# Four-layer conv stack on one core: TensorE's prices in the plan, a GpSimd share of the scan's products, and the first two images' preparation side by side

## The chip, the cores and the metric

The kernel runs on one core of a Trainium2 chip. The time is device microseconds from the start of an execution to its end. Four runs of the kernel before took 17,172.54 to 17,189.07 us, with a median of 17,181.15 us. A difference below 0.2% (about 34 us) is not told from no change here.

## The reference, cut to what matters

An image is a 128 x 56 x 56 block of float32; there are 32. Each passes four layers. Every layer normalises its input by groups of four channels and adds its result to the input.

```python
x = x + _L0(gn(x))   # attention-weighted 1x1 conv, then 3 dilated 3x3 depthwise convs, each through silu
x = x + _L1(gn(x))   # a cubic B-spline of every element, 10 coefficients
x = x + _L2(gn(x))   # linear attention over pooled 8x8 cells, then a 3x3 depthwise conv
x = x + _L3(gn(x))   # Mamba: layer norm, in-projection, short conv, selective scan, gate, out-projection

# inside _L3, for each position t and each of 256 inner channels d, 16 states n:
#   h[d,n] = exp(delta[t,d]*A[d,n]) * h[d,n] + delta[t,d]*xc[t,d] * B[t,n]
#   y[t,d] = sum_n h[d,n] * C[t,n]
```

The scan of layer 3 is the largest part, and the change touches its product `delta*xc*B`.

## The kernel before, in words

An image lies in SBUF as 128 channels x 3136 positions (tile `xt`). The positions are cut into NCH = 7 chunks of CH = 448. The scan of one chunk is cut into STEPS = 16 **steps**: DI = 2 halves of 128 inner channels, times NPAIR = 8 **pairs** of states. A step handles two states for 128 channels, as a tile of 128 partitions x 2 x 448. So an image has 112 steps and the run 3,584.

One step (class `Scan`, from line 1028) is made of these pieces:

- `b_rows`: one TensorE matmul spreads the two rows of B over the partitions, into the one PSUM buffer `pb` (pool `ps_bc`, one buffer).
- `c_rows`: the same for C. It runs for the first half alone; ScalarE copies it from PSUM to an SBUF tile `cb`, which both halves use.
- `decay`: two ScalarE exponentials write `da` to PSUM (three buffers).
- `state`: VectorE multiplies `du` (delta*xc, in SBUF) by `pb` into `h` (line 1074), then runs two scans over `h`. Tile `h` has three buffers.
- `products`: GpSimd multiplies `h` by `cb` into `hc` (two buffers); ScalarE keeps the last column of `h` in `last`.
- `add`: TensorE sums `hc` over the states into the PSUM tile `y`, two steps later.

While an image is scanned, layers 1 and 2 of the next one and layer 0 of the one after run between its steps. `Pieces` deals their generators out over the steps (`until_scan`, from line 1132, is layers 1 and 2 and the first layer norm; `first_layer`, from line 1125, is layer 0). Within a chunk, `gate` and `ssm_inputs` make the next chunk's `delta`, `du` and `xc`; the normed chunk goes through the tiles `xns` (three buffers, line 541).

The order on each engine is written out ahead by a planner (`Plan`, lines 95 to 325). Every instruction becomes a `Work` with a cost from `price` (line 163), a due time worked back from its step (`STEP` = 4.5 us for each), and what it reads and writes. `attempt` then goes through a simulated run: it takes the work that could start first on its engine, by due time among those near, and the engines' queues are issued in that order. On the chip every engine works through its own queue in order. `price` sets a float32 TensorE matmul of n columns at 1.8 ns a column and a float32r one at 0.5 ns a column.

Ahead of the loop (lines 1255 to 1262) three things are planned one after the other: layer 0 of image 0, its layers 1 and 2 with the first chunk's inputs, and layer 0 of image 1. Then a loop of five rounds follows, each with six images planned together, and a last part with two images.

All instructions are recorded through one helper, so nearly every line of the profile says L325; tiles tell them apart.

Of the kernel before, what the change touches and what calls it, by code (L numbers as in the profile page):

```python
# [19 lines left out]
P = 128  # L20
# [47 lines left out]
NB = DI * P // Q  # L68
NPAIR = NST // 2
STEPS = NPAIR * DI  # L70
AHEAD = 2
LAG = 3
FIRST, SECOND = 8, 4
# [7 lines left out]
class Work:  # L81


    __slots__ = ("engine", "calls", "reads", "writes", "cost", "bytes", "step", "ahead", "table", "due", "next",
                 "ready", "fresh")

    def __init__(self, engine, step, ahead):
        self.engine, self.step, self.ahead = engine, step, ahead
        self.calls, self.reads, self.writes = [], [], []
        self.cost = self.bytes = self.ready = self.due = 0.0  # L90
        self.table = None
        self.next, self.fresh = [], []


class Plan:
# [6 lines left out]
    RATE, LANDING = 2e5, 1.8  # L102
    TABLE = 1.28
    NEVER = 1e18
    PATIENCE = {"tensor": 0.5, "scalar": 0.9, "gpsimd": 0.6, "vector": 0.1, "sync": 0.0}

    def __init__(self, nc, tc):
# [55 lines left out]
    def price(self, w, engine, method, args, kw):  # L163

        n = args[0].free_size()
        if method == "dma_start":
            w.cost += 0.35
            w.bytes += 4 * n * args[0].partition_size()
        elif engine == "tensor":
            n = args[2].free_size() if method == "matmul" else n  # L170
            w.cost += max(0.06, n * (5e-4 if args[2].dtype == F32R else 1.8e-3))
        elif engine == "scalar":
            if method == "activation" and args[2] in (AF.Exp, AF.Tanh, AF.Ln):
                w.table = "ln" if args[2] == AF.Ln else "exp"
            columns = sum(isinstance(kw.get(k), bass.AP) for k in ("bias", "scale"))
            w.cost += 0.06 + 8.34e-4 * n + 0.09 * columns + 0.03 * (args[1].space != bass.MemoryType.PSUM)
        elif engine == "gpsimd":
            if n <= 8:
                w.cost += 0.52 if ALU.pow in args else 0.15
            else:  # L180
                slow = method != "tensor_scalar" or ALU.add not in args
                w.cost += 0.14 + n * (1.2e-3 if not slow else 2.12e-3 if method != "tensor_scalar" else 3.8e-3)
        elif method == "tensor_tensor_scan":
            w.cost += 0.11 + 2.085e-3 * n
        else:
            if method == "tensor_reduce" or method == "bn_stats":
                n = args[1].free_size()
            w.cost += 0.08 + 1.02e-3 * n
# [54 lines left out]
    def attempt(self, born, behind):  # L243
# [6 lines left out]
        left = dict(self.uses)  # L250
        free = {e: 0.0 for e in self.PATIENCE}
        ready = {e: [] for e in self.PATIENCE}
        slots, held, table, bus, first = {}, {}, None, 0.0, 0
        for name, (pool, tag, bufs) in self.tiles.items():
            slots[pool, tag] = [0.0] * bufs
            held[pool, tag] = []
# [5 lines left out]
        while len(out) < len(works):  # L262
            while done[first]:
                first += 1
            front = works[first].step + self.WINDOW
            best = None
            for e, cand in ready.items():
                for i in cand:
                    w = works[i]
                    if w.step > front:  # L270
                        continue
                    at = max(w.ready, free[e])
                    for name in w.fresh:
                        at = max(at, min(slots[self.tiles[name][:2]], default=self.NEVER))
                    if at >= self.NEVER:
                        continue
                    late = at - self.PATIENCE[e] * (w.ahead > 0)
                    if w.table and w.table != table:
                        late += 0.6

                    key = (max(late, free[e]), w.due, i)
                    if best is None or e != best[1] and at < best[3] or e == best[1] and key < best[0]:
                        best = (key, e, i, at)
            if best is None:
                full = [t for t in (self.tiles[n][:2] for n in works[first].fresh) if not slots[t]]
                behind.setdefault(first, []).append(max(born[n] for t in full for n in held[t]))
                return None
            key, e, i, at = best
            w = works[i]
            ready[e].remove(i)  # L290
            done[i] = True
            for name in w.fresh:
                t = self.tiles[name][:2]
                slots[t].remove(min(slots[t]))
                held[t].append(name)
            free[e] = at + w.cost
            if w.table:
                free[e] += self.TABLE * (w.table != table)
                table = w.table
            end = free[e]  # L300
            if w.bytes:
                bus = max(bus, end) + w.bytes / self.RATE
                end = bus + self.LANDING
            for name in self.used[i]:
                left[name] -= 1
                if not left[name]:
                    t = self.tiles[name][:2]
                    slots[t].append(end + self.HOP[e])
                    held[t].remove(name)
            for k in w.next + behind.get(i, []):  # L310
                v = works[k]
                waits[k] -= 1
                v.ready = max(v.ready, end + self.HOP[e] * (v.engine != e or e != "tensor"))
                if not waits[k]:
                    ready[v.engine].append(k)
            out.append((at, i))
        return [i for _, i in sorted(out)]

    def issue(self):
        order, works = self.order(), self.works  # L320
# [29 lines left out]
def tile_conv_stack(ctx: ExitStack, tc: tile.TileContext, out: bass.AP, x: bass.AP, w: dict):  # L350
# [12 lines left out]
    wide = pool("wide", 1)  # L363
    ssm = pool("ssm", 2)
    cbp = pool("cbp", NPAIR + 1)
    dramp = ctx.enter_context(tc.tile_pool(name="dramp", bufs=1, space=bass.MemoryType.DRAM))
    ps_mm = pool("ps_mm", 3, space=bass.MemoryType.PSUM)
    ps_bc = pool("ps_bc", 1, space=bass.MemoryType.PSUM)
# [169 lines left out]

    xts = [const.tile([P, L], F32, name=f"xt{k}") for k in range(3)]
    sts = [const.tile([P, NCH, 6], F32, name=f"st{k}") for k in range(2)]  # L540
    xns = [const.tile([P, CH + DCONV - 1], F32, name=f"xn{k}") for k in range(3)]
    dbls = [const.tile([P, CH], F32R, name=f"dbl{k}") for k in range(2)]
    xcs = [const.tile([P, DI, CH], F32, name=f"xc{k}") for k in range(2)]
    halves = [[const.tile([P, 2, CH], F32, name=f"{n}{k}") for k in range(3)] for n in ("delta", "du")]
# [444 lines left out]
    def ssm_inputs(xt, k, norm):  # L989

        dbl, xc = dbls[k % 2], xcs[k % 2]
        j, xn = k % NCH, xns[k % 3]
        for db in range(DI):
            ch = slice(db * P, (db + 1) * P)
            ps = psum()
# [16 lines left out]
            nc.vector.tensor_scalar(delta[:, db, :], ps, dtb[:, db : db + 1], 0.0, ALU.add, ALU.max)  # L1012
            yield 0.8
        nc.scalar.activation(du[:], du[:], AF.Exp, scale=-1.0)
        layer_norm(xt, xns[(k + 1) % 3], j + 1, norm if j + 1 < NCH else None, xn, du[:])
        nc.gpsimd.tensor_add(delta[:], delta[:], du[:])
        nc.gpsimd.tensor_mul(du[:], delta[:], xc[:])
        yield 4.0
# [9 lines left out]
    class Scan:  # L1028
# [3 lines left out]
        def __init__(self, xt, dst, last, k):  # L1032
            self.xt, self.dst, self.last, self.j, self.k = xt, dst, last, k % NCH, k
            self.dbl, self.xc = dbls[k % 2], xcs[k % 2]
            self.cbs, self.pbs, self.das, self.hcs = {}, {}, {}, {}

        def half(self, n):

# [16 lines left out]

        def b_rows(self, n):

            p = n % NPAIR
            self.pbs[n] = ps_bc.tile([P, 512], F32, tag="bc", name="pb")[:, :CH]
            self.both(self.pbs[n], B_ROW, p)  # L1060

        def decay(self, n):
# [3 lines left out]
            for i in range(2):  # L1066
                b = 2 * db + i
                nc.scalar.activation(self.das[n][i], delta[:, i, :], AF.Exp, scale=amat[:, b, p : p + 1])

        def state(self, n):  # L1070
            _, du = self.half(n)
            da = self.das.pop(n)
            h = ssm.tile([P, 2, CH], F32, tag="h", name="h", bufs=3)
            nc.vector.tensor_mul(h[:], du[:], self.pbs.pop(n).unsqueeze(1).to_broadcast([P, 2, CH]))
            for i in range(2):
                nc.vector.tensor_tensor_scan(
                    h[:, i, :],
# [3 lines left out]
                    ALU.mult,  # L1081
                    ALU.add,
                )
            self.h = h

        def products(self, n):
            h = self.h
            if self.j < NCH - 1:
                nc.scalar.copy(self.last[:, n, :], h[:, :, CH - 1])
            hc = ssm.tile([P, 2, CH], F32, tag="hc", name="hc", bufs=2)  # L1090
# [41 lines left out]
    def until_scan(b):  # L1132
# [4 lines left out]
        norm = carried[b % 2]  # L1137
        norm_weights(st, *norm)
        yield 5.0
        layer_norm(xt, xns[b * NCH % 3], 0, norm)  # L1140
        yield 5.0

    def first_inputs(b):
# [7 lines left out]
    class Pieces:  # L1151
# [12 lines left out]
            except StopIteration:  # L1164
                self.gen = None

        def finish(self, plan=None):
            while self.gen is not None:
                if plan is not None:
                    plan.at(plan.step + 1)  # L1170
                self.next()
            return self.taken

    xv = x.rearrange("b c l -> c b l")
# [3 lines left out]
    def images(first, count, ahead):  # L1178
# [18 lines left out]
        for b in range(count):  # L1197
# [5 lines left out]
            for j in range(NCH):  # L1203
                k = b * NCH + j
                if k == 0:
# [3 lines left out]
                        at(n, "c_rows")  # L1209
                    for n in range(2):  # L1210
                        at(n, "b_rows")
                    at(0, "decay")
                following = [gate(xns[k % 3])]
                if j + 1 < NCH:
                    following.append(ssm_inputs(xt, k + 1, carried[b % 2]))
                elif more:
# [2 lines left out]
                for n in range(STEPS):  # L1219
# [14 lines left out]
                    plan.at(g, FIRST)  # L1234
                    at(g + 2, "b_rows")
                    at(g, "state")
                    at(g + 1, "decay")
                    at(g, "products")
                    at(g + AHEAD, "c_rows")
# [14 lines left out]

    totals = [0.0, 0.0]
    plan.start()
    for b in range(2):
        totals[0] = Pieces(first_layer(xv[:, b : b + 1, :].squeeze(1), b)).finish(plan)
        if b == 0:
            totals[1] = Pieces(until_scan(0)).finish(plan)  # L1260
            Pieces(first_inputs(0)).finish(plan)
    plan.issue()
    with tc.For_i(0, B - 2, unroll) as i:
        images(i, unroll, True)
# [103 lines left out]
```

## Time and profile before

| | us |
|---|---|
| median of four runs | 17,181.15 |
| the profiled execution's own time | 17,196.77 |
| its span, first to last instruction | 17,194.7 |
| first scan product starts (the part ahead of the loop ends) | 504.9 |
| the two images behind the loop start their scans | 16,261.1 |
| the last image starts its scan | 16,766.5 |

The times of the last three rows are those at which VectorE starts the first `h<-du,pb` of the part. Between 504.9 and 16,261.1 us, 30 images take 525.2 us each on the mean. Mean granted TensorE clock: 0.886 of full speed.

In the profile, PE is TensorE's matmuls, PEld its weight loads, DVE is VectorE, ACT ScalarE, POOL GpSimd and SP the queue that issues the DMAs. A float32 matmul is two MATMUL instructions there. An operation is named out<-in by tiles: `hc<-h,cb` is the product with C. "A <- B" in a view of waits is time in which the engine of A stood idle until B ended.

### The profile page before, as it was taken

To read this page: it belongs to the slowest core of one execution; us is meant where nothing else is said; L and a number is where in the kernel's file an instruction comes from. 1 tells how busy PE (TensorE), PEld (TensorE's weight loads), DVE (VectorE), ACT (ScalarE), POOL (GpSimd) and SP (SyncE) were. 2 spreads that over 40 slices of the span, in tenths; PEclk is the share of its full clock that TensorE was granted. 3 is DMA by queue.
4 is the path that set the end of the run, shared out by engine and by line. 5 is a ranking of instruction groups with operands and counts; after the bars stand their busy time and mean duration, and the time that the engine had idled before them with its cause. 6 is when DMAs were issued, how large, how long until landed. Compare 5 with 4: busy or idle time off the path is not lost. (4 is left out here: it accounts for less than half of the span.)

```text
span 17194.7 us, 216067 instructions
## 1 busy us (share of the span) xinstructions
PE 14993.2 (87%) x68192; PEld 4864.7 (28%) x68192; DVE 14448.7 (84%) x17314; ACT 11730.0 (68%) x21127; POOL 10789.5 (63%) x6406
## 2 busy tenths in 40 slices
PE   5888998888988888988889888889888898888888
PEld 1222222222222222222222222222222222222222
DVE  2788888888888888888888888888888888888889
ACT  3666667766677666777666776667776667776675
POOL 1566666656666666666666666666666666666666
PEclk7888898989998888989889888899888999898887
DMA  4443443434433444434334434444343444343421
GB/s 106 104 96 94 101 98 85 97 88 98 106 90 85 97 95 99 99 85 97 92 93 106 94 80 96 95 102 98 86 96 90 94 106 94 84 97 93 95 54 31
DMA packets 986167, 1590.09 MB, mean 92 GB/s; under 512 B 175621, under 2 KB 611208, under 8 KB 984330
## 3 DMA queue, kind: packets, MB, share of 16 engines
q1 hardware_dynamic: 985002, 1576.06, 39.0%
q8 instruction: 548, 8.98, 0.2%
q14 instruction: 617, 5.05, 0.1%
HBM read 785.62 MB, written 173.18 MB: 56 GB/s over the span
## 5 line engine op out<-in xcount | busy, mean ns | idle before, releaser
L325 POOL TENSOR_TENSOR hc<-h,cb 128x896 f32<-128x896 f32 x3584 | 7482.2, 2093 | 5038.6 <-DVE h L325 2473.2
L325 DVE TENSOR_TENSOR_SCAN h<-da,last,h 128x448 f32<-128x448 f32 x6144 | 6807.8, 1137 | 627.8 <-ACT da L325 529.4
L325 ACT ACTIVATE da<-delta,alog 128x448 f32<-128x448 f32 x7168 | 4490.7, 633 | 2043.8 <-DVE h L325 1831.7
L325 DVE TENSOR_TENSOR h<-du,pb 128x896 f32<-128x896 f32 x3584 | 3831.7, 1069 | 428.6 <-PE pb L325 184.9
L325 PE MATMUL y<-hc,sums 128*64 128x448 f32 x14336 | 3933.0, 627 | 286.6 <-POOL hc L325 282.0
L325 PE MATMUL pb<-dbl,sel 64*128 64x448 f32 x3584 | 1842.9, 514 | 626.3 <-DVE h L325 585.3
L325 PE MATMUL mm<-xn,winT 128*128 128x448 f32 x3584 | 1786.0, 606 | 172.7 <-DVE sz L325 129.9
L325 PE MATMUL mm<-stack,dsT 96*32 96x448 f32 (+1 forms) x16128 | 1868.2, 573 | 59.9 <-DMA stack<-onesd 27.6
L325 ACT ACTIVATE hats<-stack,bia,scl 128x448 f32<-128x448 f32 x2688 | 1894.4, 755 | 12.8 <-DVE bia L325 10.0
L325 PE MATMUL mm<-hats,wspl 128*32 128x448 f32 x12544 | 1476.6, 574 | 130.7 <-DVE xt L325 68.5
L325 PEld LDWEIGHTS pb<-dbl,sel 64*128 64x128 f32 x3584 | 714.7, 199 | 2985.6 <-DVE h L325 1870.9
L325 PEld LDWEIGHTS y<-hc,sums 128*64 128x64 f32 x14336 | 800.1, 146 | 2064.6 <-issue 969.5
L325 ACT ACTIVATE t<-mm 128x448 f32<-128x448 f32 x1568 | 816.5, 536 | 788.7 <-PE mm L325 783.9
L325 ACT COPY cb<-mm 128x448 f32<-128x448 f32 x1792 | 927.9, 529 | 568.8 <-PE mm L325 471.5
L325 PE MATMUL mm<-dbl,sel 64*128 64x448 f32 x1792 | 874.1, 517 | 477.9 <-ACT cb L325 139.9
L325 ACT ACTIVATE hats<-hats,one 128x1344 f32<-128x1344 f32 x896 | 1261.3, 1408 | 1.2
L325 ACT COPY last<-h 128x2 f32<-128x2 f32 x3072 | 579.3, 189 | 817.0 <-DVE h L325 783.0
L325 DVE TENSOR_TENSOR_SCAN h<-da,h 128x448 f32<-128x448 f32 x1024 | 1062.9, 1071 | 54.8 <-ACT da L325 46.6
L325 POOL TENSOR_TENSOR xt<-xt,g 128x448 f32<-128x448 f32 x672 | 765.1, 1139 | 336.3 <-DVE g L325 331.1
L325 PEld LDWEIGHTS mm<-xn,winT 128*128 128x128 f32 x3584 | 614.2, 199 | 1029.2 <-issue 664.5
L325 PEld LDWEIGHTS mm<-stack,dsT 96*32 96x32 f32 (+1 forms) x16128 | 427.8, 112 | 1123.0 <-issue 862.5
L325 DVE SCALAR_TENSOR_TENSOR g<-t,mm 128x448 f32<-128x448 f32 x672 | 409.4, 609 | 398.9 <-ACT t L325 396.1
(187 smaller groups left out, 15888.4 us busy)
## 6 DMA issues: line engine op xcount, KB each, us to landing
stack<-padded SPq DMA_DIRECT2D x2688, 264.0 KB
stack<-xt SPq DMA_DIRECT2D x3584, 56.0 KB
delta<-delta SPq DMA_DIRECT2D x1792, 112.0 KB
du<-du SPq DMA_DIRECT2D x1792, 112.0 KB
padded<-yc SPq DMA_DIRECT2D x224, 264.0 KB
padded<-yc SPq DMA_DIRECT2D x256, 231.0 KB
xt<-x_dram SPq DMA_DIRECT2D x224, 224.0 KB
out_dram<-xt SPq DMA_DIRECT2D x224, 224.0 KB
```

What stands on the lines that cost most here:

```text
L325: call()
```

## The change

Four things change together.

1. `ASIDE = (4,)`: for pair 4 of the eight, `b_rows` makes B's rows once for both halves, in a general PSUM buffer, and ScalarE copies them to an SBUF tile `bb` (new pool, one buffer). GpSimd then multiplies `du` by `bb` for that pair, in place of VectorE's multiply of `du` by `pb`. These are two of a chunk's 16 products.
2. The product leaves `state` for a method of its own, `inputs`. It is listed for step g+1 right behind `state` of step g, so for every pair it is recorded, and due, one step earlier.
3. TensorE's prices: a float32r matmul costs 0.16 us more, a float32 one 0.02 us + 1.75 ns a column, both with full clock. `Plan.run` keeps a load for each window of 3.413 us and lets TensorE work at half speed in a window that follows one with too little load.
4. Layer 0 of image 1 is no longer planned behind the rest of the part ahead of the loop, but dealt out between the pieces of `until_scan(0)`.

The tiles `xns` go from three to two, which makes room for `bb`. The core of the diff:

```diff
+ASIDE = (4,)
+    GATE, BUSY = 3.413, 1.27
@@ Plan.price
-            w.cost += max(0.06, n * (5e-4 if args[2].dtype == F32R else 1.8e-3))
+            w.load += n * (1.9e-4 if args[2].dtype == F32R else 7.5e-4 * 2) * args[-1 if method != "matmul" else 1].partition_size() / P
+            w.cost += 0.16 + 5e-4 * n if args[2].dtype == F32R else max(0.22, 0.02 + 1.75e-3 * n)
@@ Plan.attempt
-            free[e] = at + w.cost
+            free[e] = self.run(at, w, loads) if e == "tensor" else at + w.cost
+    def run(self, at, w, loads):
+        left = w.cost
+        while left > 0.0:
+            k = int(at / self.GATE)
+            speed = 1.0 if loads.get(k - 1, 0.0) >= self.BUSY else 0.5
+            stay = min((k + 1) * self.GATE + 1e-9 - at, left / speed)
+            loads[k] = loads.get(k, 0.0) + stay * speed * w.load / w.cost
+            at, left = at + stay, left - stay * speed
+        return at
@@ tiles
+    bbp = pool("bbp", len(ASIDE))
-    xns = [const.tile([P, CH + DCONV - 1], F32, name=f"xn{k}") for k in range(3)]
+    xns = [const.tile([P, CH + DCONV - 1], F32, name=f"xn{k}") for k in range(2)]
@@ Scan.b_rows
-            p = n % NPAIR
+            db, p = divmod(n, NPAIR)
+            if p in ASIDE:
+                if db == 0:
+                    ps = psum()
+                    self.both(ps, B_ROW, p)
+                    self.bbs[p] = bbp.tile([P, CH], F32, tag="bb", name="bb")
+                    nc.scalar.copy(self.bbs[p][:], ps)
+                return
@@ Scan
+        def inputs(self, n):
+            _, du = self.half(n)
+            h = self.hs[n] = ssm.tile([P, 2, CH], F32, tag="h", name="h", bufs=3)
+            if n % NPAIR in ASIDE:
+                nc.gpsimd.tensor_mul(h[:], du[:], self.bbs[n % NPAIR][:].unsqueeze(1).to_broadcast([P, 2, CH]))
+            else:
+                nc.vector.tensor_mul(h[:], du[:], self.pbs.pop(n).unsqueeze(1).to_broadcast([P, 2, CH]))
         def state(self, n):
-            _, du = self.half(n)
-            h = ssm.tile([P, 2, CH], F32, tag="h", name="h", bufs=3)
-            nc.vector.tensor_mul(h[:], du[:], self.pbs.pop(n).unsqueeze(1).to_broadcast([P, 2, CH]))
+            h = self.hs[n]
@@ Pieces
-        def finish(self, plan=None):
+        def finish(self, plan=None, beside=None):
+            start = beside and beside.taken - self.taken / 2
...
+                while beside and beside.gen is not None and beside.taken - start < self.taken / 2:
+                    beside.next()
@@ images
                     at(g, "state")
+                    at(g + 1, "inputs")
                     at(g + 1, "decay")
@@ ahead of the loop
-    for b in range(2):
-        totals[0] = Pieces(first_layer(xv[:, b : b + 1, :].squeeze(1), b)).finish(plan)
-        if b == 0:
-            totals[1] = Pieces(until_scan(0)).finish(plan)
-            Pieces(first_inputs(0)).finish(plan)
+    layer0s = [Pieces(first_layer(xv[:, b : b + 1, :].squeeze(1), b)) for b in range(2)]
+    totals[0] = layer0s[0].finish(plan)
+    totals[1] = Pieces(until_scan(0)).finish(plan, layer0s[1])
+    Pieces(first_inputs(0)).finish(plan, layer0s[1])
+    layer0s[1].finish(plan)
```

## The prediction

> **What bounds the kernel now.** I read the page's engine totals first. TensorE (PE) and VectorE (DVE) are nearly level, and neither is full.
>
> ```profile
> PE 14993.2 (87%) x68192; PEld 4864.7 (28%) x68192; DVE 14448.7 (84%) x17314; ACT 11730.0 (68%) x21127; POOL 10789.5 (63%) x6406
> ```
>
> An average hides stages, so next I cut an image in the middle of the loop (the 14th) into its seven chunks, at the first scan of each, and asked for busy time in these stretches. Columns: stretch and length, then busy us of PE, PEld, DVE, ACT, POOL, the granted TensorE clock, DMA share, GB/s.
>
> ```profile
> 7333.10:7398.10 65.00, 49.67 (x161) 16.28 (x162) 59.55 (x78) 42.62 (x79) 44.06 (x25) 0.79 0.28 71
> 7398.10:7477.40 79.30, 63.42 (x253) 20.17 (x250) 67.43 (x85) 60.42 (x108) 47.53 (x30) 0.84 0.21 50
> 7477.40:7558.60 81.20, 75.97 (x361) 21.69 (x361) 64.57 (x72) 70.76 (x124) 58.08 (x35) 0.90 0.44 104
> 7558.60:7630.10 71.50, 64.45 (x363) 20.04 (x355) 62.74 (x74) 61.00 (x109) 53.23 (x33) 1.00 0.49 112
> 7630.10:7709.90 79.80, 71.48 (x325) 28.93 (x322) 66.97 (x82) 44.61 (x86) 43.15 (x27) 0.81 0.31 71
> 7709.90:7792.30 82.40, 81.19 (x452) 25.14 (x450) 69.89 (x81) 44.91 (x91) 46.10 (x27) 1.00 0.62 147
> 7792.30:7857.40 65.10, 57.61 (x233) 18.40 (x233) 59.44 (x70) 41.08 (x68) 44.96 (x29) 0.90 0.46 103
> ```
>
> So the bound moves: VectorE in chunks 1 and 7 (92% and 91% busy), TensorE in chunk 6 (99%, at full clock), and no engine alone in chunks 2 to 5 (VectorE 80 to 88%, waiting in turn on the others). GpSimd is never over 75%. The waits say the same: GpSimd mostly waits for VectorE's scans or for a free `hc`, and VectorE's largest wait is for ScalarE's `da`.
>
> ```profile
> POOL hc L325 <- DVE h L325: 2473.2, 1249, 6.9
> POOL hc L325 <- PE y L325: 1866.5, 804, 12.4
> ...
> DVE h L325 <- ACT da L325: 576.0, 440, 4.4
> ```
>
> Last, the part ahead of the loop. Layer 0 of image 0 ends at about 134 us; its layers 1, 2 and first inputs run to about 398; layer 0 of image 1 fills the rest up to the first scan at 504.9.
>
> ```profile
> 134.00:398.00 264.00, 166.09 (x747) 53.45 (x747) 46.07 (x100) 124.92 (x165) 42.99 (x38) 0.67 0.23 57
> 398.00:505.00 107.00, 74.15 (x526) 23.36 (x526) 22.95 (x41) 19.61 (x37) 28.85 (x26) 0.80 0.90 204
> ```
>
> **Part 1: two images ahead of the loop.** The second stretch, 107 us, moves beside the first. Does it fit? TensorE's work at full clock is 166.09 x 0.67 + 74.15 x 0.80 = 171 us, ScalarE's 145, the DMA engines' 0.23 x 264 + 0.90 x 107 = 157, all below 264. By their yields, layer 0 counts 90 units and `until_scan` 212, and one unit is dealt out for two, so all of layer 0 is dealt out by 180 of 212. SP's transfers of layer 0 (the same stack loads, in the same number) join a queue that was nearly idle. The first stretch is a chain of latencies (ScalarE's functions, a slow-clock matmul, VectorE, and again), and in-order queues will hold it up here and there. I take 107 less 17 for that: **-90 us**. Ends: -40, if more than half of it comes back as waits, and -120, if the busier TensorE also gets more clock than 0.67.
>
> **Part 2: VectorE's relief and what pays for it.** The rows:
>
> ```profile
> L325 POOL TENSOR_TENSOR hc<-h,cb 128x896 f32<-128x896 f32 x3584 | 7482.2, 2093 | 5038.6 <-DVE h L325 2473.2
> L325 DVE TENSOR_TENSOR h<-du,pb 128x896 f32<-128x896 f32 x3584 | 3831.7, 1069 | 428.6 <-PE pb L325 184.9
> L325 PE MATMUL pb<-dbl,sel 64*128 64x448 f32 x3584 | 1842.9, 514 | 626.3 <-DVE h L325 585.3
> L325 ACT COPY cb<-mm 128x448 f32<-128x448 f32 x1792 | 927.9, 529 | 568.8 <-PE mm L325 471.5
> ```
>
> A chunk loses 2 VectorE products, 2 x 1.069 = 2.14 us, and 1 of 16 `pb` matmuls net (two go, one for `bb` comes), 0.51 us. It gains one ScalarE copy, 0.53 us by `cb`'s row, and two GpSimd products of the same shape as `hc`, 2 x 2.093 = 4.19 us. In all VectorE sheds 448 x 1.069 = 479 us and GpSimd takes 938.
>
> What is on the path differs by chunk. Chunks 1 and 7: VectorE sets the pace, all 2.14 counts. Chunk 4 (88%): 1.5. Chunks 2 and 5 (85 and 84%): about half, 1.1 each. Chunk 3, where ScalarE stands at 87% and TensorE at 94%: 0.4. Chunk 6 is TensorE's: its 0.5. Sum 4.3 + 1.5 + 2.2 + 0.4 + 0.5 = 8.9 us an image. Against it stands ScalarE's copy, 0.5 in chunk 3 alone and hidden where ScalarE is at 55 to 85%; if that cover went, 3.7 an image.
>
> GpSimd also disturbs VectorE. `dm<-mv,mg`, on one column, takes 139 ns in the median, 520 on the mean and up to 1,783; where it overlaps a GpSimd operation its mean is 1,462, elsewhere 137. Its likes (`vv`, `attr`, `pooled`, `ab`, `att`) together lose about 166 us in the run. GpSimd's busy time grows by 9%, so 9% more of that: 14 us, 0.5 an image. The Trainium skill has the rule (SBUF — State Buffer, "SBUF: two separate sides"): VectorE and GpSimd take one port pair by turns, for a whole instruction, when VectorE reads two SBUF inputs. By the rule alone every GpSimd microsecond is a possible block and the change is bad; but the products and scans take one input from PSUM, and the scans' spread (1,097 to 1,153 ns over the run, with GpSimd busy or not) shows none of it. By it the sum would still be the 14 us.
>
> Net 8.9 - 0.5 - 0.5 = 7.9 an image, over 31 images 245, and in the last image, where VectorE alone is pressed, 7 x 2.1 = 15: **-260 us**. Ends: 0, if it is all swallowed by other waits, and -479.
>
> **Part 3: a new wait.** VectorE's scan of pair 4 waits for a GpSimd product that stands in GpSimd's in-order queue behind `hc` products, and these behind a free `hc` or a side addition. Behind the scan on VectorE stand the next product and all side work, so ScalarE's `da` and TensorE's `pb` wait too. In time for it: `du` and `bb` are ready steps earlier; the `h` buffer comes free with `hc` of three steps before; two steps (9.3 us) ask GpSimd for three such products, 6.3 us, and about 2 x 0.9 of side work, 8.1 in all. No row shows this wait. The nearest is VectorE's product waiting for `hc` to free `h`: 73 us in the run, 62 times, 1.2 us each. Ends: 0, and a whole GpSimd operation each time, 448 x 2.09 = +936. I take 1.2 us for one in twenty of the 448: **+27 us**.
>
> **Part 4: the plan's prices and the earlier product.** They change no instruction, only the order. In an image (14,497 to 15,019 us) VectorE stood idle 72 us, 38 of them because a TensorE result came later than the order assumed, directly or through ScalarE (`g<-t`, `xt<-mm`, `h<-pb`, `delta`, `sz`, `rden` and so on). A plan that knows TensorE at half clock can place these consumers later; all of it would be 31 x 38 = -1,180. On the other side, a wrong order costs; how much an order's luck is worth is seen in the loop's images, whose orders are the same in every round: from first scan to first scan they take 520.0 to 526.3 us (the last of each round aside): +-3 us, +-100 over the run. I take -2 an image, nearest to that row: **-62 us**. The Trainium skill (TensorE: Matmul & The Clock Gate, "What's actually happening") says the clock's window runs free of the kernel. If so the planned windows lie beside the real ones and this part is 0; the spread just named would agree.
>
> **At nothing:** `xns` with two buffers. The norm that overwrites a buffer waits for the `gate` of the same chunk, dealt out some six steps before, about 28 us; without that cover GpSimd's queue, `hc` with it, would stand until TensorE reads. `bb`'s one buffer is rewritten some seven steps after its last reader. The earlier listing of the products adds none.
>
> **Sum:** -90 - 260 + 27 - 62 = -385. The profiled execution took 17,196.8, so 16,812; it lies 15.6 above the median of the runs, so **16,796 us**.
>
> **The rivals.**
> - *More comes through* (chance 0.20). VectorE's relief counts whole (-479), part 1 gives -90, and better prices 5 us an image (-155): -724, 16,457. For it: VectorE has the most work that no clock can speed up. Against: 99% TensorE in chunk 6.
> - *Only the part ahead of the loop gains* (0.18). Chunks are set by TensorE and by waits in turn, VectorE's 2 us only lengthen its idle time: 17,181 - 90 = 17,091. For it: in that image's chain of waits TensorE holds half of the time and VectorE's `h` 15%.
> - *GpSimd's product comes late* (0.12, slower). In its queue it stands behind an `hc` that waits for `y`, which is GpSimd's second largest wait. The gains without part 3 are 412 us, so the point of decision is 412/448 = 0.92 us a product. At 1.25 us, 560 - 412 = +148: 17,329.
> - *Nothing to measure* (0.05): part 1 gives its low end and the loop a little back, 17,160.
>
> The forecast itself has 0.45, with 16,650 to 16,950 as its own range. The range for 8 in 10 leaves out about half of the first rival and most of the slower one: 16,450 to 17,215. Faster by over 0.2% (34 us, about what a measurement tells from no change): 0.45 + 0.20 + 0.18 = 0.83; within 0.05; slower 0.12.
>
> **What would show it.** The first scan starts near 415 us instead of 505 (part 1). Chunks 1 and 7 of an image fall from 65 to about 63 us, chunk 6 stays at 82 (part 2). A wait of VectorE's `h` for a GpSimd product, absent now, stays below 50 us (part 3). `g<-t`, `xt<-mm` and `h<-pb` waits fall somewhat, and the clock stays near 0.89 (part 4). The prediction is wrong if chunk 6 or the mixed chunks move by over 5 us either way, or if that new wait is in hundreds of microseconds.

## The result, and the profile after

The changed kernel took 17,202.91 us (median of 40 runs) against 17,179.94 us before (60 runs): the ratio is 1.0013, with a 95% interval from 1.0009 to 1.0017. That is below the 0.2% that was to count, but on the slow side: three parts that were each meant to gain gave nothing together. The profiled execution's span is 17,208.2 us, so span and median agree.

The engine totals of the changed kernel, in the page's form:

```profile
PE 14938.3 (87%) x67968; PEld 4900.1 (28%) x67968; DVE 14084.5 (82%) x16866; ACT 11830.9 (69%) x21351; POOL 11698.2 (68%) x6854
```

VectorE's busy time fell by 364 us and GpSimd's grew by 909. The products by themselves did as worked out: VectorE's `h<-du,pb` fell by 474 us and GpSimd's `h<-du,bb` took 938. But other operations of VectorE ran 110 us longer, and VectorE's idle time, span less busy, grew from 2,746 to 3,124 us. All of the 364 became waiting.

The part ahead of the loop, cut at the same times as before (the first scan product now starts at 441.5 us instead of 504.9):

```profile
134.00:398.00 264.00, 195.05 (x1277) 65.43 (x1269) 55.60 (x103) 126.75 (x178) 64.97 (x56) 0.76 0.56 128
398.00:443.00 45.00, 20.05 (x43) 9.61 (x44) 6.03 (x14) 17.18 (x24) 8.66 (x9) 0.67 0.17 39
```

The first stretch now holds layer 0 of image 1 as well: 1,277 matmuls instead of 747, at a clock of 0.76 instead of 0.67. What it was to hide is hidden, and 45 us of the old work are left over behind it. So 63 us are won here.

The seven chunks of the same image as before (the 14th), with the same columns:

```profile
7317.10:7389.70 72.60, 54.85 (x166) 18.02 (x166) 61.40 (x77) 45.06 (x83) 48.42 (x27) 0.74 0.26 66
7389.70:7466.60 76.90, 64.58 (x263) 19.94 (x259) 62.73 (x81) 63.80 (x114) 55.33 (x33) 0.87 0.24 62
7466.60:7545.80 79.20, 72.48 (x344) 21.79 (x342) 62.16 (x71) 67.80 (x119) 58.50 (x36) 0.87 0.42 97
7545.80:7620.20 74.40, 67.46 (x360) 21.00 (x359) 61.00 (x71) 63.07 (x113) 57.53 (x35) 0.93 0.47 107
7620.20:7696.10 75.90, 71.19 (x325) 29.17 (x325) 64.29 (x80) 44.86 (x87) 49.60 (x30) 0.84 0.34 79
7696.10:7774.70 78.60, 78.16 (x445) 24.53 (x444) 66.30 (x80) 43.72 (x89) 46.99 (x27) 1.00 0.62 145
7774.70:7838.20 63.50, 56.87 (x238) 18.27 (x234) 59.15 (x68) 41.64 (x69) 50.30 (x31) 0.92 0.48 111
```

The first chunk is the one to look at. It was VectorE's, at 92%; it went from 65.0 to 72.6 us, and VectorE is idle for 11 us of it. Chunks 2, 3, 5, 6 and 7 gained about 2 to 4 us, chunk 4 lost 3. This image as a whole even took 3 us less than before (521.1 against 524.3), so it does not show the loss; on the mean over the 30 images of the loop chunk 1 rose from 65.4 to 73.5 us, and it stands at 70.4 in e4 below, without a product on GpSimd. Over the loop, from its first scan to the first scan behind it, the time rose from 15,755 to 15,838 us: +83, which eats the 63. (The times 16,261.1 and 16,766.5 in the table of the kernel before are those of first scans; the products before them start at 16,257.2 and 16,765.3.)

VectorE's waits (us, times, longest), first before, then in the changed kernel:

```profile
DVE h L325 <- PE pb L325: 184.9, 176, 3.6
...
DVE sz L325 <- PE y L325: 126.3, 112, 5.1
...
DVE h L325 <- POOL hc L325: 73.3, 62, 1.5
```

```profile
DVE h L339 <- ACT da L339: 732.9, 593, 5.8
...
DVE h L339 <- PE pb L339: 333.2, 256, 5.0
...
DVE sz L339 <- PE y L339: 272.3, 145, 5.4
DVE h L339 <- POOL hc L339: 229.5, 184, 3.5
...
DVE h L339 <- POOL h L339: 45.1, 53, 1.9
```

The last line is the wait that the prediction was afraid of, VectorE's scan for GpSimd's product, and it is small. The line above it stood at 73.3 us before. It is VectorE's own product that waits for GpSimd's `hc`, that is, for a free buffer of `h`. This line gave theory D, which was put on record before e5. Two other waits grew by as much, by some 150 us each: the product's for `pb`, and that of `sz`, the gate, for `y`, the sum of `hc`.

**Theory D.** In the plan, the GpSimd product needs only `du`, `bb` and a free `h` buffer, all there early, and GpSimd has idle time. So the planner places it far ahead of its scan. From then on it holds one of the three `h` buffers, and VectorE works with two or one. To see it, the k-th `h<-du,bb` was matched with the k-th scan of pair 4: from the end of the product to the start of the scan 12.5 us pass on the mean; for the second half of a chunk's steps the median is 16.6 us, for the first half only 1.1. The last image shows it best, since no other image's layers run beside the scan there. This is its second chunk in the timeline of the changed kernel (start, length, what, idle before):

```profile
16830.41 2.08 POOL L339 TENSOR_TENSOR h<-du,bb 128x896 f32<-128x896 f32 x1
...
16838.44 2.19 DVE L339 TENSOR_TENSOR_SCAN h<-da,last,h 128x448 f32<-128x448 f32 x2
...
16840.78 2.08 POOL L339 TENSOR_TENSOR hc<-h,cb 128x896 f32<-128x896 f32 x1 [6.12 <-DVE h L339]
...
16842.89 1.09 DVE L339 TENSOR_TENSOR h<-du,pb 128x896 f32<-128x896 f32 x1 [0.38 <-POOL hc L339]
...
16844.01 2.19 DVE L339 TENSOR_TENSOR_SCAN h<-da,last,h 128x448 f32<-128x448 f32 x2
...
16846.38 2.08 POOL L339 TENSOR_TENSOR hc<-h,cb 128x896 f32<-128x896 f32 x1 [3.52 <-DVE h L339]
```

The product made at 16,830.41 is the one of step 12; its scan starts at 16,878.7, 46 us later. The product of step 4 was made at 16,824.0, for a scan at 16,850.6. Two of three buffers are taken, so product, scan and `hc` follow each other one by one. The step from scan to scan takes 5.6 us, where such steps without the held buffers take 3.6.

**Rivals**, on record before e1. A: the order that the new prices make costs what the relief gains. B: the relief is swallowed by other waits wherever it falls. C: GpSimd's product disturbs by its own 2.09 us in front of `hc`.

### The profile page after: what moved, and what is told of

Its sections match the earlier page's. It is cut to its first block, busy times and chain, and to the rows that moved or that the text cites. A ratio compares the mean times of both kernels' runs of the same rounds, so it can differ in the third digit from the quotient of the medians.

```text
span 17208.2 us, 214516 instructions
## 1 busy us (share of the span) xinstructions
PE 14938.3 (87%) x67968; PEld 4900.1 (28%) x67968; DVE 14084.5 (82%) x16866; ACT 11830.9 (69%) x21351; POOL 11698.2 (68%) x6854
## 5 line engine op out<-in xcount | busy, mean ns | idle before, releaser
L339 PE MATMUL y<-hc,sums 128*64 128x448 f32 x14336 | 4049.7, 649 | 401.4 <-POOL hc L339 398.9
L339 DVE TENSOR_TENSOR h<-du,pb 128x896 f32<-128x896 f32 x3136 | 3357.6, 1071 | 648.7 <-PE pb L339 333.2
L339 PE MATMUL pb<-dbl,sel 64*128 64x448 f32 x3136 | 1620.2, 517 | 686.5 <-DVE h L339 651.3
L339 PE MATMUL mm<-dbl,sel 64*128 64x448 f32 x2016 | 975.7, 528 | 476.7 <-DVE g L339 102.8
L339 PEld LDWEIGHTS pb<-dbl,sel 64*128 64x128 f32 x3136 | 629.8, 201 | 2578.7 <-DVE h L339 1516.9
L339 POOL TENSOR_TENSOR h<-du,bb 128x896 f32<-128x896 f32 x448 | 938.0, 2094 | 213.5 <-DMA out_dram<-xt 69.5
L339 PEld LDWEIGHTS mm<-dbl,sel 64*128 64x128 f32 x2016 | 390.9, 211 | 1568.4 <-issue 300.0
```

The source lines that it names most:

```text
L339: call()
```

## The experiments

All times are medians. "Half clock" is the time that TensorE's clock stood at half in the profiled run, summed from the clock's records.

| run | what | us | half clock, us |
|---|---|---|---|
| | before | 17,180 | 3,932 |
| | changed | 17,203 | 4,319 |
| e1 | before + interleaved start | 17,142 | 3,905 |
| e2 | before + new prices | 17,189 | 3,987 |
| e3 | before + GpSimd products, earlier listing | 17,338 | 4,449 |
| e4 | changed, no GpSimd products | 17,101 | 4,082 |
| e5 | changed, products in step order | 16,973 | 3,491 |
| e6 | e4 with two `h` buffers | 17,301 | 4,150 |
| e7 | e4 with the rule of e5 | 17,105 | 4,058 |
| e8 | before + earlier listing | 16,845 | 3,215 |
| e9 | e5 with the old prices | 17,300 | 4,678 |
| e10 | e5, GpSimd one step early | 17,156 | 4,060 |
| e11 | e5 with two pairs on GpSimd | 17,243 | 4,679 |
| e12 | before, one price 3% off | 17,173 | 3,860 |
| e13 | e8, one price 3% off | 17,371 | 4,112 |
| e14 | changed, one price 3% off | 17,218 | 4,192 |
| e15 | e5, one price 3% off | 16,943 | 3,768 |
| e16 | e4, one price 3% off | 17,128 | 3,975 |
| e17 | e9, one price 3% off | 17,377 | 4,853 |
| e18 | e8 + interleaved start | 16,725 | 3,027 |

### The parts one by one (e1 to e4)

e1 takes the change's part ahead of the loop into the kernel before:

```diff
-    for b in range(2):
-        totals[0] = Pieces(first_layer(..., b)).finish(plan)
...
+    totals[1] = Pieces(until_scan(0)).finish(plan, layer0s[1])
```

> The kernel before with the interleaved part ahead of the loop alone. In the changed kernel the first scan product starts at 441.5 us instead of 504.9, and this part is planned by itself, so both theories expect the first scan 55 to 75 us earlier (the plan's prices differ between the two, which may shift it by some us), the loop's rounds at 3,147 to 3,158 us as before, and a time of -55 to -75 us, about 17,115.

Ratio 0.9979 (0.9970 to 0.9988), -38 us. The first scan came 69 us earlier. Its VectorE, ScalarE and GpSimd queues from the first scan on hold the same operations in the same order as before, and yet its loop took 15,784 instead of 15,755 us. Both expectations held for the part itself and were off by 17 us for the whole.

e2 puts `price`, `run` and `free[e] = self.run(...)` of the change into the kernel before.

> The kernel before with TensorE's new prices and the modelled clock alone; no instruction changes but the order. Theory A (the order that the new prices make costs what VectorE's relief gains): slower by 200 us or more, 17,380 and up. Theory B (the relief is swallowed by other engines' waits wherever it falls): within 60 us of before. Theory C (GpSimd's product disturbs): within 60 us of before, or faster as forecast by up to 62.

Ratio 1.0007 (0.9998 to 1.0016): no difference. A fell; the prices alone make no worse order, nor a better one.

e3 takes GpSimd's products, the earlier listing and two `xns`, and leaves the prices and the start as they were.

> The kernel before with GpSimd's products, the earlier listing of all products and two norm buffers; old prices, old part ahead of the loop. Theory A: faster by about 260, 16,920. Theory B: within 60 us of before. Theory C: slower by 80 us or more, 17,260 and up, with a wait of VectorE or TensorE on GpSimd that the kernel before has not.

Ratio 1.0091 (1.0076 to 1.0106), +158 us. Theory C expected this, but e8 and e13 below have the same kernel without GpSimd's products at 16,845 and 17,371 us, so with the old prices GpSimd's part cannot be told from the order's. e4 takes the GpSimd products out of the changed kernel:

```diff
-ASIDE = (4,)
+ASIDE = ()
```

> The changed kernel with no pair on GpSimd (an empty list of pairs): interleaved start, new prices, earlier listing and two norm buffers stay, VectorE makes all products again. Theory A: slower than the changed kernel by the relief, 260, so 17,460. Theory B: within 60 us of the changed kernel, 17,140 to 17,260. Theory C: faster than the changed kernel by 80 or more, 17,120 or less.

Ratio 0.9950 (0.9936 to 0.9963), 17,101 us. So 102 us of the changed kernel come with GpSimd's products. A and B fell; C remained, and D, which was stated after this run, gives the same.

### Too early or too long (e5 to e7, e10)

e5 adds one rule to the planner, and no instruction:

```diff
         behind = {}
+        hs = sorted(born[n] for n, (pool, tag, _) in self.tiles.items() if n in born and (pool, tag) == ("ssm", "h"))
+        for i, k in zip(hs, hs[1:]):
+            behind.setdefault(i, []).append(k)
```

> The changed kernel, with one rule more in the plan: a product of du is placed behind the product of the step before it, on whichever engine. Instructions are the same. Theory D (in the changed kernel the GpSimd product is placed up to 12 steps early, sits in one of the three h buffers all that time and leaves VectorE two or one): the lead of the GpSimd product falls from 12.5 us on the mean to under 5, VectorE's waits of h for hc fall from 230 us to under 90, and the time falls below the version without GpSimd products (17,101), to 16,950 to 17,080. Theory C2 (GpSimd's own 2.09 us, in front of hc, make y and the side work late wherever they stand): 17,180 to 17,240, about the changed kernel, and VectorE's waits for hc stay.

Ratio 0.9874 (0.9859 to 0.9889), 16,973 us. GpSimd does the same 448 products, now 0.66 us ahead of their scans on the mean, and the kernel is 230 us faster than the changed one and 128 faster than e4. VectorE's waits in e5:

```profile
DVE h L342 <- POOL hc L342: 156.3, 124, 4.1
...
DVE h L342 <- POOL h L342: 98.5, 132, 1.7
```

The wait for `hc` fell from 230 only to 156, not under 90 as expected, where e4 without GpSimd's products has 114; the wait for the product itself rose. VectorE's wait of `sz` for `y` fell from 272 to 72 (e14, the changed kernel in another order, has 111). The time was as D expected and not as C2, the form of C in the expectation.

Two rivals of the held buffer are left. An early product also stands in front of an `hc` in GpSimd's queue and so makes `y` late, and the rule of e5 takes that away too. And other operations of VectorE run longer in the changed kernel: of the 228 us between the two profiled spans, VectorE's busy time makes up 95 (14,084.5 against 13,989.6, with the same instructions) and its idle time 133.

The last image, cut from its first scan to the first scan of its seventh chunk, shows the cost without other images' layers. Before, changed kernel, e5:

```profile
16766.50:17131.30 364.80, 316.31 (x768) 96.39 (x767) 332.62 (x349) 206.76 (x420) 234.59 (x124) 0.76 0.15 34
```

```profile
16768.20:17141.30 373.10, 300.90 (x767) 95.05 (x766) 325.62 (x339) 213.83 (x430) 262.18 (x138) 0.78 0.14 34
```

```profile
16567.20:16917.50 350.30, 291.74 (x762) 90.78 (x762) 319.99 (x337) 214.03 (x428) 259.32 (x137) 0.80 0.15 36
```

With the product too early the six chunks take 373.1 us. They take 373.1 and 379.7 in e14 and e3 too, the other two versions that place it early, and 346 to 365 in all kernels that do not. So in the last image the cost of placing it early shows in every order. The gain does not: in step order the chunks take 350.3 us in e5 but 360.1 in e15, and without GpSimd's products 364.8 before, 354.7 in e4 and 350.4 in e12. In e5 the third step's scan in the second chunk, which started 5.6 us after the second's in the changed kernel, starts 3.6 us after it.

e6 measures the price of a buffer by itself, with VectorE making all products:

```diff
-            h = self.hs[n] = ssm.tile([P, 2, CH], F32, tag="h", name="h", bufs=3)
+            h = self.hs[n] = ssm.tile([P, 2, CH], F32, tag="h", name="h", bufs=2)
```

> The version without GpSimd products (17,101), with two buffers of h in place of three: the price of one buffer by itself, all the time. Theory D: slower by 200 us or more, since the changed kernel lacks a buffer in some 2 to 5 of 8 steps and loses 100. Theory C2: three buffers are more than VectorE needs, within 40 us of 17,101.

Ratio 1.0072 (1.0059 to 1.0086), 17,301 us: one buffer less, all the time, costs 200 us in this one order, and the wait that was the theory's sign is there without a single GpSimd product:

```profile
DVE h L339 <- POOL hc L339: 548.2, 340, 4.0
```

e7 puts the rule of e5 into e4:

> The version without GpSimd products (17,101), with the rule that products are placed in step order. VectorE's products are made nearly in order without it, so both theories expect within 40 us of 17,101; it shows how much the rule changes by itself.

Ratio 0.9954 (0.9940 to 0.9967), 17,105 us. The queues of VectorE, ScalarE and GpSimd are the same as in e4, operation by operation: the rule does nothing where VectorE makes all products. What it does in e5 it does to the GpSimd product.

e10 loosens the rule: the GpSimd product stands behind the product two steps before.

```diff
-        for i, k in zip(hs, hs[1:]):
-            behind.setdefault(i, []).append(k)
+        for i, k in zip(hs, hs[1:]):
+            if self.works[k].engine == "vector":
+                behind.setdefault(i, []).append(k)
+        for i, k in zip(hs, hs[2:]):
+            if self.works[k].engine == "gpsimd":
+                behind.setdefault(i, []).append(k)
```

> The in-order version (16,973) with a GpSimd product behind the product two steps before it, not one: it may be one step early. The in-order version has a new wait of VectorE for GpSimd's product, 98 us in 132 waits. If that wait is what now holds back the relief, it falls below 40 us and the time falls by 20 to 60, to 16,910 to 16,950; if the step for which a buffer is held costs as much, the time stays within 20 of 16,973 or rises.

Ratio 0.9985 (0.9976 to 0.9994), 17,156 us: a rise, as the second expectation allowed, but by 183 us. The lead is 3.9 us, and the wait for the product 82 us, hardly less. With the new prices the time lies the higher the longer the lead: 16,973 at 0.66 us, 17,156 at 3.9, 17,203 at 12.5. But e10 is one order, and VectorE's wait for `hc`, the sign of a held buffer, is 128 us in it, below e5's 156; its six chunks of the last image take 349.7 us. So the runs do not show that its loss is the buffer's.

### Prices, listing and luck (e8, e9, e11 to e18)

e8 is e3 without GpSimd products: the product stands in `inputs`, one step earlier, and two `xns`.

> The kernel before with products listed one step earlier and two norm buffers alone: no GpSimd product, old prices, old part ahead of the loop. The version with all but GpSimd's products took 79 us less than before, of which the interleaved start alone gives 38. If the earlier listing is worth something by itself, this run shows -20 to -60 (17,120 to 17,160); if the rest of the 79 was the new prices together with the earlier listing, or the luck of the order, it lies within 20 of 17,180.

Ratio 0.9807 (0.9794 to 0.9821), 16,845 us. This was a surprise, outside both expectations: the part that the prediction had at nothing gave -335. e9 takes the new prices out of e5:

> The in-order version (16,973) with TensorE's old prices and no modelled clock: what the prices are worth where no h buffer is lost. As forecast in the prediction: slower by about 62, 17,035. If prices do not matter beyond the luck of the order (the prices alone gave +9): 16,930 to 17,010.

Ratio 1.0073 (1.0060 to 1.0087), 17,300 us: neither expectation held. e11 gives GpSimd a second pair:

```diff
-ASIDE = (4,)
+ASIDE = (2, 5)
-    cbp = pool("cbp", NPAIR + 1)
+    cbp = pool("cbp", NPAIR)
```

> The in-order version with two of eight pairs (2 and 5) on GpSimd, and one buffer less for the copies of C to make room. If VectorE's relief still counts as in the first pair (132 us from 17,105 to 16,973): 16,840 to 16,900. If GpSimd, at 69% with one pair and some 74% with two, now makes hc late, or ScalarE's further copies count: 16,973 or more.

Ratio 1.0036 (1.0022 to 1.0050), 17,243 us, within the second expectation. VectorE's wait for GpSimd's products is 282 us there, and GpSimd is at 73%. Since it also has one `cb` buffer less, its loss is not split further.

By then the versions lay 500 us apart and no single cause ordered them. So the planner's scatter was measured: each of these kernels changes one price by 3%, which reorders thousands of queue entries and alters no instruction.

```diff
-            w.cost += max(0.06, n * (5e-4 if args[2].dtype == F32R else 1.8e-3))
+            w.cost += max(0.06, n * (5e-4 if args[2].dtype == F32R else 1.75e-3))
```

(With the new prices: 0.02 + 1.8e-3 * n in place of 0.02 + 1.75e-3 * n.)

> The kernel before with TensorE's float32 price 1.75 in place of 1.8 ns a column: the same instructions in another order, for no reason. It measures how much an order's luck moves the time. If orders of equal merit lie close: within 40 us of 17,180. If the plan is chaotic: 100 us or more off, to either side.

> The version with products listed one step earlier (old prices, 16,845), with the same change of the float32 price. If the earlier listing itself is worth 335 us: within 60 us of 16,845. If it was a lucky order: 16,950 or more, near 17,100.

> The changed kernel with a float32 price of 1.80 in place of 1.75 ns a column beside its 0.02. If its time is what its parts cost: within 60 us of 17,203. If it was an unlucky order: 17,100 or less (or a lucky one: 17,300 or more).

> The in-order version (16,973) with a float32 price of 1.80 in place of 1.75. If placing the products in order is what gains against the changed kernel: within 60 us of 16,973, and some 200 below the changed kernel with the same price. If it was luck: as near to 17,200 as to 16,973, or above.

e12: ratio 0.9995 (0.9986 to 1.0005), 17,173. e13: 1.0110 (1.0093 to 1.0127), 17,371, which is 526 us above its twin e8. e14: 1.0019 (1.0010 to 1.0029), 17,218, 15 from the changed kernel. e15: 0.9862 (0.9846 to 0.9879), 16,943, 30 from e5. So e8 is a lucky order, e13 an unlucky one, and the earlier listing has no price of its own that can be read from them. The changed kernel and its in-order version kept their distance: 230 us at the one price, 275 at the other.

> The version without GpSimd products (17,101) with a float32 price of 1.80 in place of 1.75. With the changed kernel (17,203 and 17,218) and the in-order version (16,973 and 16,943) each measured at two prices, this is the second point of their common base. If GpSimd's products early cost some 100 and in order gain some 130 whatever the order: 17,060 to 17,140. If 17,101 was itself a lucky or unlucky order, 17,000 or less or 17,200 or more, and then neither number holds.

Ratio 0.9967 (0.9954 to 0.9981), 17,128. The base without GpSimd products is 17,101 and 17,128, so GpSimd's products cost 102 and 90 us as the change places them, and gain 128 and 185 in step order.

> The in-order version with the old prices (17,300) and a float32 price of 1.75 in place of 1.8. If the old prices spoil it: within 60 us of 17,300. If that was an unlucky order: 17,200 or less, and the prices' part cannot be told.

Ratio 1.0114 (1.0098 to 1.0129), 17,377, 77 us from e9 and outside both expectations. With the old prices the in-order rule helps in neither order: e3, which places the product early and has the old start, took 17,338.

> The fastest loop so far (products listed one step earlier, old prices, 16,845) with the interleaved part ahead of the loop. That part is planned by itself, so the loop's order stays: 16,845 less the 38 that it gave the kernel before, 16,790 to 16,825.

Ratio 0.9736 (0.9723 to 0.9750), 16,725 us, the fastest version, 2.8% below the changed kernel. It gained 120 us from e8 and not 38, more than expected; its loop holds the same operations in the same order on VectorE, ScalarE and GpSimd, and ran 15,375 instead of 15,420 us.

## Why the prediction was wrong, point by point

- **Part 1, -90:** the mechanism was right; the term was too large. The first scan came 63 us earlier (69 in e1), and e1 gained 38: its loop, the same order started at another moment, ran 29 us longer in the profiled executions. Why an earlier start lengthens the loop is open.
- **Part 2, -260:** the products left VectorE as worked out (474 us), but 110 came back as longer operations of VectorE, where the prediction had 14. In the changed kernel none of the rest came out as time. Placed in step order the products on GpSimd gave 128 and 185 us with the new prices, so even then the chunk by chunk estimate was too large, by a factor of 2.0 and 1.4. For the last image it had 15 us: from its first scan to the end the span shrank from 428.2 to 412.9 in e5, but e12 with all products on VectorE has 413.7 and e15 in step order 422.8, so that agreement is luck.
- **Part 3, +27, is the step that failed.** It asked whether GpSimd's product comes too late, found that "the `h` buffer comes free with `hc` of three steps before", and stopped. The wait it priced is indeed small, 45 us. What it missed is that a product that is ready early will be placed early. The runs put GpSimd's share at +102 and +90 us in place of 27 - 260 = -233, and with the new prices the step order alone takes 230 and 275 us off. That the early product costs by the buffer that it keeps is the best supported account, not a shown one. For it are VectorE's wait for `hc` (230 and 277 us in the changed kernel and e14, 114 in e4 and in e16), e6, and the last image. The waits for `pb` and `y`, the late `hc` and VectorE's longer operations have not been told from it.
- **Part 4, -62:** the prices alone gave +9 us, within nothing; the image-to-image spread from which the term was taken (+-100 a run) was too small a measure for the scatter of orders, which reached 526 us between e8 and e13.
- **At nothing:** the earlier listing and the two `xns`. By their instructions they are nothing, but by the order they gave -335 in one version and +191 in its twin.
- **The rivals:** the slower one named the right engine and the opposite fault.
- **The signs:** chunk 7 fell to 63.5 us as expected, but chunk 1 rose. `g<-t` and `xt<-mm` waits fell (396 to 334 and 386 to 311 us), `h<-pb` rose by 148. Neither sign of being wrong appeared: in the image looked at, chunks 2 to 6 moved by less than 4 us, and the new wait was 45. The signs looked for a late product, so an early one passed them.

With the new prices the account is: start -38, prices and listing together -14 to -41 (e4 and e16 against e1), GpSimd +102 and +90. Its sum must come out, since each part is measured from the one before; what supports it is that the parts are near each other in two orders. Against that stands that one of the six pairs of orders measured moved by 526 us, and the other five by 7 to 77. Left open: why the in-order rule fails with the old prices (17,300 and 17,377). GpSimd's lead is short there (0.78 and 0.88 us), so an early product is not what holds them. TensorE's clock stands at half for 4,678 and 4,853 us, with e11's 4,679 the three longest, but the runs do not say whether that is cause or effect. That the other engines' orders also differ between the changed kernel and e5 means that 230 and 275 us are not the buffer's price alone.

## What to carry to other kernels

When work moves to an idle engine, ask what it holds from the moment it starts, not only whether it is done in time: an early producer in a small ring of buffers can take room from the engine that it was to relieve, and stands in front of what follows it in its own queue. In a kernel whose order a planner makes, tie such work to the order of its ring; here that gained with the new prices and not with the old. And before crediting a change with a percent, disturb a price that should not matter and see how far the time moves by itself.

## What the runs showed of the hardware that was not expected

The same order ran 29 us slower (before and e1) and 45 us faster (e8 and e18) in the loop, and in each of these pairs the loops differ, as far as is known, by nothing but a start some 70 us earlier. These are single profiled executions, and the executions of one kernel spread by some 30 us. Over all runs the time goes with how long TensorE's clock stood at half: 3,027 us in the fastest, 4,853 in the slowest, though not strictly (e13 has 4,112 at 17,371).

Of VectorE's small operations, `dm<-mv,mg`, which the prediction looked at, rose in the median from 139 to 330 ns (198 in e5), but hardly on the mean: 520 ns before, 543 in the changed kernel.

```profile
L339 DVE TENSOR_TENSOR dm<-mv,mg x128: 131/330/1352, 28.7 to 16703.8; 128x1 f32<-128x1 f32 x128
```

Others rose far more. `ctr<-ident,rs`, before and in the changed kernel:

```profile
L325 DVE TENSOR_SCALAR ctr<-ident,rs x32: 257/259/288, 367.2 to 16704.7; 128x128 f32<-128x128 f32 x32
```

```profile
L339 DVE TENSOR_SCALAR ctr<-ident,rs x32: 259/1712/1728, 400.3 to 16707.7; 128x128 f32<-128x128 f32 x32
```

In the changed kernel 30 of the 32 `ctr` start while GpSimd's `hc` runs, and end some 80 ns after it. Before and in e5, 30 of the 32 overlap an `hc` too, but start ahead of it, and take some 260 ns. So for this pair an overlap costs VectorE time when GpSimd's operation has started first, and a new order of the two brings or removes that cost.
